# Graph attention on one core: which PSUM bank holds what, and the order of the readers of PE

## The chip, the core and the metric

The kernel runs on one core of one Trainium2 chip. The metric is the device time in microseconds. Three runs of the kernel before give a median of 2156.45 us (2150.37 to 2159.99).

## What is computed

A graph has N = 12500 nodes with 128 features and E = 212500 edges, sorted by their destination, each with 128 features of its own. There are 8 heads of 16 features.

```python
Q, K, V = x @ WQ, x @ WK, x @ WV            # (N, 8, 16) each
Eh = edge_attr @ WE                          # (E, 8, 16)
score = K[src] * Q[dst] / sqrt(16) * Eh
score = exp(clip(score.sum(-1), -5, 5))      # (E, 8, 1)
wV = segment_sum(V[src] * score, dst)        # (N, 8, 16)
Z = segment_sum(score, dst)                  # (N, 8, 1)
h = x + (wV / (Z + 1e-6)).reshape(N, 128)
h = (h - mean(h)) * rsqrt(var(h) + 1e-5) * gamma + beta   # over the nodes
out = layernorm(x + h)                       # over the features, no weights
```

## The kernel before

**Tiles.** Edges lie in tiles of 128, one per partition. A group holds two windows of 4 tiles; the last group holds 3 and 2. There are 208 groups (`NG`). Since the edges are sorted, the destinations of one window fall into 64 consecutive nodes, which begin at `BASE[g][h]`. `hx` holds x, transposed, in SBUF for the whole run; it is overwritten by h as groups end.

**Head.** PE multiplies x with the K and V weights, and the products go to a table `kvd` in DRAM (`table_rows`, L605). The first 8 groups don't wait for this table: for them GpSimd gathers rows of x (64 gathers), and K and V are computed on the spot, for groups 0 to 3 during the head, for groups 4 to 7 in the main loop (`project_main`, L277 and L284). All others take their rows of K and V from `kvd`: 1585 indirect DMAs on GpSimd's queue (L198), one for each tile, into 8 slots that hold one group each. The message of a group frees its slot. In 12 groups one tile is instead fetched row by row from SyncE's queue (L231). Gathers are let go one by one: `pace` makes a gather wait for a certain DVE instruction, seven in each group, and an eighth goes when a slot comes free.

**One group in the main loop.** The order in which the functions are called is the order on each engine, as nothing is scheduled by a tool (`manual_schedule`). For group g:

- `ehqe` (two groups ahead): PE computes Eh (L500, bank `ps_e`) and Q at the edges (L503, bank `ps_q`): Q is split into three bf16 parts and multiplied with a one-hot matrix. ACT copies Eh to SBUF (L506).
- `both` (one ahead): DVE multiplies the two (L512). `turn_back`: PE transposes the product (L520, `ps_t`).
- `products`: DVE multiplies by K (L529); `scores` adds up 16 features of a head (L536); `clip_exp` clips (L541), and ACT writes the exponential twice, to PSUM for DVE (L543) and to SBUF (L544).
- `onehot` (L460 to L463): DVE compares node numbers with an iota that lies in PSUM. `message` (L550): DVE multiplies V by the exponential.
- `gather_sum` (one behind): PE adds the messages of each node by the one-hot (L565), with a carry from the window before (L564). `sums_out`: ACT copies the sums (L570).
- `denom`, `recip`, `attn` (two behind): DVE divides (L574, L577, L581). `add_x`: PE turns the result and adds x (L587, L588), ACT writes it to `hx` (L590). `bn_part`: statistics over nodes (L593).
- `q_window`, `q_mm`, `q_hi`, `q_mid`, `q_lo` (two to four ahead): ACT cuts 64 nodes out of `hx` (L449), PE computes Q (L480), ACT and DVE split it (L484, L488, L489, L492).

**Banks.** PSUM has 8 banks here: two each of `ps_e`, `ps_q` and `ps_t`, one `ps_m` (`small_ps`) and one `ps_a` (`sum_ps`). `ps_m` holds Q in two alternating places, the update of x, and a place for odd jobs. `ps_a` holds the sums, the iota and the exponentials of two groups. Semaphores guard a bank as a whole: an instruction that reads or writes it waits for those of other engines that touched the bank before it.

**End.** After the loop, which runs two rounds past the last group for its updates, `norm_factors` makes scale and shift (`ab`). All engines then come to a branch (L724): if the input doesn't fit the assumptions, a slow path (`any_order`) is computed instead; here it is skipped. Then comes the last stage, 25 tiles of 512 nodes: `residual` (h scaled and shifted, plus x; DVE at L764, or GpSimd, tile 0 on DVE, L767 and L768), `centred` (PE turns the tile and subtracts the mean, L776 and L778), `variance` (ACT, Square with a sum for each block of 128 nodes, L796, or bn_stats on DVE for three tiles, L791 and L793; square root on ACT, L798), `scaled` (DVE, L806 and L812; output on SyncE's queue, L814).

Of the kernel before, what the change touches and what calls it, by code (L numbers as in the profile page):

```python
# [17 lines left out]
H = 8  # L18
# [44 lines left out]
def gnn_kernel(  # L63
# [41 lines left out]
    small_ps = psp.tile([P, 4, P], F32, name="ps_m", bufs=1)  # L105


    sum_ps = psp.tile([P, 4 * P], F32, name="ps_a", bufs=1)
    iota_ps = sum_ps[:, W:W + P]

    def exp_ps(g):
        c = W + P + (g % 2) * G * H
        return sum_ps[:, c:c + G * H].rearrange("p (t h) -> p t h", h=H)
# [46 lines left out]
    iota = consts.tile([P, P], F32, name="iota")  # L160
    nc.vector.tensor_copy(iota, io_i)
# [4 lines left out]
    nc.vector.tensor_scalar(ident, iota, piota, None, op0=OP.is_equal)  # L166
# [6 lines left out]
    nc.vector.memset(ones, 1.0)  # L173
    eps = consts.tile([P, 1], F32, name="eps")
# [151 lines left out]
    def place(r):  # L326
        nc.vector.tensor_copy(vw(rel, r), vw(rel_i, r))
        nc.vector.tensor_tensor(vw(rel, r), vw(rel, r), bc(base_f, r), op=OP.subtract)
        end = ustarts[r[0]] + (r[1] - r[0]) * r[2]
        for t in range(ustarts[r[0]], end, P):  # L330
            n = min(P, end - t)
            ps = small_ps[:, 3, :]
            nc.tensor.transpose(ps[:n], rel[:, t:t + n], ident)
            row = wp.tile([P, P], BF16, name="relrow", bufs=2)
            nc.vector.tensor_copy(row[:n], ps[:n])
            nc.scalar.dma_start(relT[t:t + n, :], row[:n])
# [22 lines left out]

    def shift_tiles():  # L360

        t = rows.tile([P, 4, 2 * P], F32, name="t", bufs=4)
        shift3, rows3 = t[:, 0, :65], t[:65, 1, :P // 2].bitcast(BF16)
        nc.vector.memset(rows3, 0.0)
        nc.vector.memset(shift3, 0.0)
        for r in (0, 32, 64):
            nc.vector.memset(rows3[r:r + 1, :], 1.0)
        return rows3, shift3
# [5 lines left out]
    def check(i):  # L374
# [17 lines left out]
        elif i == len(runs) + 1:  # L392
# [4 lines left out]
            ps = small_ps[:, 3, :]  # L397
# [45 lines left out]
    def q_window(g):  # L443
# [3 lines left out]
        XW[g] = wp.tile([P, P], F32, name="xw", bufs=7)  # L447
# [30 lines left out]
    def q_mm(g):  # L478
        PQ[g] = small_ps[:, g % 2, :]
        nc.tensor.matmul(PQ[g], XW[g], w_q, start=True, stop=True)  # L480
# [13 lines left out]
    def ehqe(g):  # L494

        QE[g], WT[g] = [], []
        for h, (a, b) in enumerate(halves(g)):
            eh = psp.tile([P, U * P], F32, name="ps_e", bufs=2)[:, :(b - a) * P]
            qe = psp.tile([P, U * P], F32, name="ps_q", bufs=2)[:, :(b - a) * P]
            nc.tensor.matmul(eh, w_e, EA[g][:, a:b, :].rearrange("p a b -> p (a b)"), start=True, stop=True)  # L500
            r = slice(h * WN, (h + 1) * WN)
            for k in range(3):
                nc.tensor.matmul(qe, Q3[g][r, k, :], OT[g][r, :(b - a) * P], start=(k == 0), stop=(k == 2))  # L503
            QE[g].append(qe)
            t = wp.tile([P, U * P], F32, name="wt", bufs=2)
            nc.scalar.activation(t[:, :(b - a) * P], eh, AF.Copy)  # L506
            WT[g].append(t)

# [30 lines left out]
    def clip_exp(g):  # L539
# [5 lines left out]
        if g == NG - 1:  # L545
            nc.scalar.activation(warm, eps, AF.Sqrt)
# [38 lines left out]
    def add_x(g):  # L585
        ps = small_ps[:, 2, :]
        nc.tensor.matmul(ps, AT[g], ident, start=True, stop=False)  # L587
        nc.tensor.matmul(ps, ident, XW[g], start=False, stop=True)  # L588
        for h in (0, 1):
            nc.scalar.activation(hx[:, ds(BASE[g][h], WN)], ps[:, h * WN:(h + 1) * WN], AF.Copy)  # L590
# [67 lines left out]
    ehqe(1)  # L658
    within(load, 2)
# [11 lines left out]
    for g in range(NG + 2):  # L671
# [5 lines left out]
        within(both_halves, g + 1)  # L677
        within(gather_sum, g - 1)
        within(q_mm, g + 3)
        within(scores, g)  # L680
        within(clip_exp, g)
        within(sums_out, g - 1)
        within(q_hi, g + 3)
# [4 lines left out]
        if g + 1 < nxg and g + 1 not in SLOT:  # L688
            for _ in project_main(g + 1):
                pass  # L690
        within(turn_back, g + 1)
        within(add_x, g - 2)
        within(q_window, g + 4)
        within(turned_onehot, g + 3)
        within(onehot, g)
        within(ehqe, g + 2)
        within(message, g)
        within(q_mid, g + 3)
# [9 lines left out]
        if g == NG // 2:  # L708
            three = shift_tiles()
# [3 lines left out]
        for w in (2 * g - 3, 2 * g - 2):  # L713
            for j in due.get(w, []):
                bn_part(j)
                done.add(j)
    for j in range(NCH):
# [6 lines left out]
    with tc.If(flag[0] != 0):  # L724
        any_order(tc, N, T, hx, xT, src, dst, eaT, w_q, w_e, kvd, dram, ident, stats, cuts)
        norm_factors()


    fin = ctx.enter_context(tc.tile_pool(name="fin", bufs=3))
    fps = ctx.enter_context(tc.tile_pool(name="fps", bufs=8, space=bass.MemoryType.PSUM))  # L730
    Y, PY, V = {}, {}, {}
# [3 lines left out]
    if len(pairs[-1]) > 1 and width(NY - 1) < B4:  # L735
        pairs[-1:] = [[NY - 2], [NY - 1]]

# [4 lines left out]
    rows3, shift3 = three  # L742


    nc.vector.tensor_copy(shift3[:, 0:65:32], ab[:, 1:2].to_broadcast([P, 3]))
    row_ps = fps.tile([P, 4, P], F32, name="ps_y", bufs=8)[:65, 0, :]
    nc.tensor.matmul(row_ps, shift3, cent, start=True, stop=True)
    row = fin.tile([65, P], BF16, name="row", bufs=1)
    rest = fin.tile([65, P], F32, name="rest", bufs=1)

    def shift_row():
        nc.vector.tensor_copy(row, row_ps)  # L752
        nc.vector.tensor_sub(rest, row_ps, row)
        nc.vector.tensor_copy(row[32:33], rest[32:33])
        nc.vector.tensor_copy(row[64:65], rest[64:65])
        nc.vector.tensor_sub(row[64:65], rest[64:65], row[64:65])

    def residual(i):

        c, n = i * B4, width(i)  # L760
        Y[i] = fin.tile([P, B4], F32, name="y", bufs=6)
        y, h = Y[i][:, :n], hx[:, c:c + n]
        if i in on_vector:
            nc.vector.scalar_tensor_tensor(y, h, ab[:, 0:1], XR[i][:, :n], op0=OP.mult, op1=OP.add)  # L764
        else:
            eng = nc.gpsimd if i else nc.vector
            eng.tensor_scalar(y, h, ab[:, 0:1], ab[:, 1:2], op0=OP.mult, op1=OP.add)  # L767
            eng.tensor_tensor(y, y, XR[i][:, :n], op=OP.add)  # L768
        if i == 0:
            shift_row()  # L770

    def centred(i):
        PY[i] = fps.tile([P, 4, P], F32, name="ps_y", bufs=8)
        whole = i in on_vector
        if whole:
            nc.tensor.matmul(PY[i], rows3, row[:, None, :].to_broadcast([65, 4, P]), start=True, stop=False)  # L776
        for k, m in blocks(i):
            nc.tensor.matmul(PY[i][:m, k, :], Y[i][:, k * P:k * P + m], cent, start=not whole,  # L778
                             stop=(k == 3 or not whole))

    def variance(p):
        v = fin.tile([P, 2, 4, 2], F32, name="v", bufs=4)
        V[p[0]] = v
        sq = fin.tile([P, P], F32, name="sq")
        if blocks(p[-1])[-1][1] < P:
            nc.vector.memset(v, 1.0)
        for h, i in enumerate(p):
            if i in by_stats:
                bn = fin.tile([P, 4, 6], F32, name="bn", bufs=2)
                for k in range(4):  # L790
                    nc.vector.bn_stats(bn[:, k, :], PY[i][:, k, :])  # L791
                for k in range(4):
                    nc.vector.bn_aggr(v[:, h, k, :], bn[:, k, :])  # L793
            else:
                for k, m in blocks(i):
                    nc.scalar.activation(sq[:m], PY[i][:m, k, :], AF.Square, scale=P ** -0.5,  # L796
                                         accum_out=v[:m, h, k, 1:2])
        nc.scalar.activation(spread(p), spread(p), AF.Sqrt, bias=eps)  # L798

    def spread(p):  # L800
        nb = len(blocks(p[-1]))
        return V[p[0]][:, :len(p), :nb, 1]

    def scaled(p):
        v = V[p[0]]
        nc.vector.reciprocal(spread(p), spread(p))  # L806
        o = fin.tile([P, 2, 4, P], F32, name="o")
        for h, i in enumerate(p):
            bl = blocks(i)
            c, fb = i * B4, sum(m == P for _, m in bl)  # L810
            if fb:
                nc.vector.tensor_tensor(o[:, h, :fb, :], PY[i][:, :fb, :],  # L812
                                        v[:, h, :fb, 1:2].to_broadcast([P, fb, P]), op=OP.mult)
                nc.sync.dma_start(out[c:c + fb * P, :].rearrange("(c p) d -> p c d", p=P), o[:, h, :fb, :])  # L814
            for k, m in bl[fb:]:
                nc.vector.tensor_scalar(o[:m, h, k, :], PY[i][:m, k, :], v[:m, h, k, 1:2], None, op0=OP.mult)
                nc.sync.dma_start(out[c + k * P:c + k * P + m, :], o[:m, h, k, :])

    on_vector = {i for i in range(2, NY, 2) if width(i) == B4}
    by_stats = {i for i in range(5, NY, 8) if width(i) == B4}  # L820
    for i in range(len(pairs) + 4):
        for f, k in ((residual, i), (centred, i - 1), (variance, i - 1), (scaled, i - 2)):
            if 0 <= k < len(pairs):
                if f in (residual, centred):
# [136 lines left out]
```

## Time and profile before

| what | value |
|---|---|
| median of three runs | 2156.45 us |
| profiled execution, whole | 2865.58 us |
| its span, first to last instruction | 2863.8 us |
| granted clock of PE, mean | 0.804 |
| DMA, mean rate | 135 GB/s |
| groups of the main loop | 208 |
| first products (L529) | at 101.2 us |
| last products | at 2795.1 us |
| gathers from `kvd` (L198) | 1585, 949 ns each, first at 106.8 us |

In the prediction's lines, a group stands as: line, engine, operation, output<-inputs, shape, count, then busy time and mean duration, then idle time of the engine just before these instructions and what ended most of it. In a timeline the first number is the start in us from the span's begin, the second the duration, and the bracket holds idle time before it and its releaser. In the table by stretches, each row has the stretch, its length, then the busy time of PE, weight loads (PEld), DVE, ACT and POOL (GpSimd), with counts, then granted clock, DMA share and GB/s. PE's ends are modelled, its starts are recorded.

### The profile page before, as it was taken

Reading aid. Unit: us, or ns where it says so; the run is one execution under the profiler, and the core shown is the slowest. Engines: PE = TensorE matmul, PEld = TensorE weight load, DVE = VectorE, ACT = ScalarE, POOL = GpSimd, SP = SyncE. Lnnn points to the kernel's source line nnn. Section 1 sums busy time; section 2 is a strip of 40 time slices with the busy share of each in tenths; the row PEclk is TensorE's granted clock in tenths of the full one; section 3 lists DMA queues with packets and bytes.
Section 4 is the critical chain, followed back from the end, with each engine's and each line's share of the span. In section 5 each row is a group of like instructions: output and inputs, shape, how many; then the busy total and the mean of one; then the engine's idle time right before and its main releaser. Section 6 shows DMA issues by size and latency. Waiting matters only on the chain. (4 is left out here: it accounts for less than half of the span.)

```text
span 2863.8 us, 37931 instructions
## 1 busy us (share of the span) xinstructions
PE 2215.0 (77%) x9339; PEld 1237.7 (43%) x9339; DVE 1666.6 (58%) x3597; ACT 683.0 (24%) x2539; POOL 1594.8 (56%) x1681
## 2 busy tenths in 40 slices
PE   7778778867787777877778777877877777877895
PEld 6444444433443443444434444433434444444454
DVE  3346556555655655655556655555555565656586
ACT  2132222222222222222222222222222222222235
POOL 6634555555555555555556555565556555655524
PEclk8788777788868878788987778788788787878797
DMA  7643444444444444444444444444444444444353
GB/s 244 200 122 115 132 118 144 131 136 124 134 115 137 135 135 131 135 120 130 127 136 129 135 126 137 128 137 126 128 133 138 127 139 134 126 144 130 115 178 94
DMA packets 179738, 386.84 MB, mean 135 GB/s; under 512 B 41838, under 2 KB 96151, under 8 KB 179511
## 3 DMA queue, kind: packets, MB, share of 16 engines
q0 software_dynamic: 78128, 212.05, 25.7%
q1 hardware_dynamic: 98038, 169.83, 19.3%
q10 hardware_dynamic: 3345, 2.48, 0.3%
q8 instruction: 77, 1.26, 0.2%
q14 instruction: 150, 1.23, 0.1%
HBM read 364.57 MB, written 19.63 MB: 134 GB/s over the span
## 5 line engine op out<-in xcount | busy, mean ns | idle before, releaser
L198 POOL DMA_INDIRECT slot<-kvd,srcs x1585 | 1504.1, 949 | 1137.2 <-DVE oh L463 322.2
L565 PE MATMUL ps_a<-msg,oh 128*128 128x136 f32 (+1 forms) x3322 | 643.1, 341 | 17.0 <-issue 11.7
L500 PE MATMUL ps_e<-ea,w_e 128*128 128x512 f32 x832 | 598.6, 810 | 2.5 <-DMA ea<-eaT 2.5
L565 PEld LDWEIGHTS ps_a<-msg,oh 128*128 128x128 f32 (+1 forms) x3322 | 501.4, 195 | 221.3 <-issue 173.7
L512 DVE TENSOR_TENSOR wt<-wt,ps_q 128x512 f32<-128x512 f32 x416 | 279.3, 683 | 375.7 <-remote 123.5
L587 PE MATMUL ps_m<-ident,at 128*128 128x128 f32 x416 | 120.6, 380 | 439.5 <-ACT q L484 281.0
L503 PE MATMUL ps_q<-ot,q 64*128 64x512 bf16 x1248 | 433.8, 465 | 0.0
L460 DVE TENSOR_TENSOR oh<-ps_a,rel_i 128x512 f32<-128x512 f32 x208 | 142.7, 686 | 444.9 <-ACT os L570 329.2
L506 ACT ACTIVATE wt<-ps_e 128x512 f32<-128x512 f32 x416 | 242.3, 591 | 396.9 <-PE ps_e L500 215.3
L520 PE MATMUL ps_t<-ident,wt 128*128 128x128 f32 x1661 | 239.8, 288 | 103.8 <-DVE wt L512 97.3
L503 PEld LDWEIGHTS <-q 64*128 64x128 bf16 x1248 | 96.0, 104 | 516.1 <-issue 485.6
L543 ACT ACTIVATE ps_a<-s 128x64 f32<-128x64 f32 x208 | 47.4, 228 | 1101.0 <-remote 555.3
L587 PEld LDWEIGHTS ps_m<-ident,at 128*128 128x128 f32 x416 | 78.5, 236 | 480.0 <-ACT q L484 315.0
L529 DVE TENSOR_TENSOR p<-slot,ps_t 128x512 f32<-128x512 f32 (+1 forms) x408 | 257.6, 672 | 11.2 <-remote 10.6
L536 DVE TENSOR_REDUCE s<-p 128x64 f32<-128x1024 f32 x208 | 251.5, 1209 | 0.0
L520 PEld LDWEIGHTS ps_t<-ident,wt 128*128 128x128 f32 x1661 | 198.7, 148 | 118.8 <-DVE wt L512 109.0
L550 DVE TENSOR_TENSOR msg<-slot,ps_a 128x1024 f32<-128x1024 f32 (+1 forms) x204 | 244.6, 1199 | 0.0
L500 PEld LDWEIGHTS ps_e<-ea,w_e 128*128 128x128 f32 x832 | 160.4, 240 | 123.9 <-issue 120.3
L590 ACT ACTIVATE hx<-ps_m 128x64 f32 x416 | 93.6, 225 | 436.1 <-PE ps_m L588 153.2
L488 DVE SCALAR_TENSOR_TENSOR qr<-ps_m,q 128x128 f32<-128x128 f32 x208 | 59.3, 285 | 224.2 <-ACT hx L590 208.6
L449 ACT ACTIVATE xw<-hx 128x64 f32 x416 | 84.1, 248 | 92.4 <-ACT hx L590 66.6
L588 PE MATMUL ps_m<-xw,ident 128*128 128x128 f32 x416 | 103.0, 339 | 0.0
(119 smaller groups left out, 1584.5 us busy)
## 6 DMA issues: line engine op xcount, KB each, us to landing
ea<-eaT SPq DMA_DIRECT2D x207, 512.0 KB
rb<-relT SPq DMA_DIRECT2D x414, 64.0 KB
slot<-kvd,srcs POOLq DMA_INDIRECT x1585
byrow<-kvd SPq DMA_DIRECT2D x1536, 1.0 KB
kvd<-t SPq DMA_DIRECT2D x24, 512.0 KB
slot<-xT SPq DMA_DIRECT2D x24, 256.0 KB
out<-o SPq DMA_DIRECT2D x24, 256.0 KB
hx<-xT SPq DMA_DIRECT2D x11, 512.0 KB
```

The lines of the kernel that those rows point to most:

```text
L198: return nc.gpsimd.indirect_dma_start(out=out, out_offset=None, in_=table, in_offset=bass.IndirectOffsetOnAxis(ap=srcs[:, e:e + 1], axis=0))
L460: nc.vector.tensor_tensor(one, iota_ps[:, None, :].to_broadcast([P, n, P]), r[:, :n, None].to_broadcast([P, n, P]), op=OP.is_equal)
L500: nc.tensor.matmul(eh, w_e, EA[g][:, a:b, :].rearrange("p a b -> p (a b)"), start=True, stop=True)
L503: nc.tensor.matmul(qe, Q3[g][r, k, :], OT[g][r, :(b - a) * P], start=(k == 0), stop=(k == 2))
L506: nc.scalar.activation(t[:, :(b - a) * P], eh, AF.Copy)
L512: pace(nc.vector.tensor_tensor(t, t, QE[g][h], op=OP.mult))
L520: nc.tensor.transpose(ps[:, j, :], WT[g][h][:, j * P:(j + 1) * P], ident)
L529: step = nc.vector.tensor_tensor(PR[g][:, c:d, :], KV[g](c, d, 0), PW[g][i][:, c - a:d - a, :], op=OP.mult)
L536: pace(nc.vector.tensor_reduce(SS[g][:, :n, :], PR[g][:, :n, :].rearrange("p t (h d) -> p t h d", d=DH), axis=AX.X, op=OP.add))
L550: nc.vector.tensor_tensor(MSG[g][:, a:b, :P].rearrange("p t (h d) -> p t h d", d=DH), KV[g](a, b, P).rearrange("p t (h d) -> p t h d", d=D ...
L565: nc.tensor.matmul(AGG[g][WN if j >= n else 0:], OH[g][j], MSG[g][:, j, :], start=(j == 0), stop=(j == n - 1))
L587: nc.tensor.matmul(ps, AT[g], ident, start=True, stop=False)
```

## The change

In PSUM, iota and exponentials move from `ps_a` to `ps_m`, and the odd jobs from `ps_m` to `ps_a`; Q has one place instead of two, next to the update of x. `ps_a` then holds only the sums and, seldom, an odd job. The calls in the loop get another order. `add_x` is cut in two (PE's part and ACT's part, `x_out`) and comes a group later, at the head of the round; `onehot` is one group ahead, after the message; `project_main` and `turn_back` come before the scores; the sums' copy comes after Q's copy. `ehqe` issues both Eh products first. The two rounds past the last group are replaced by updates written out. The last stage is made a function that runs before the branch, and again inside it if the slow path was taken. In it, tile 0 is computed in two halves on ACT and DVE, eight tiles have their squares added by DVE (`by_reduce`) and none uses bn_stats, and the shift row is one fp32 row instead of three bf16 ones.

```diff
-    iota_ps = sum_ps[:, W:W + P]
+    iota_ps, spare_ps = small_ps[:, 2, :], sum_ps[:, W:W + P]
     def exp_ps(g):
-        c = W + P + (g % 2) * G * H
-        return sum_ps[:, c:c + G * H].rearrange("p (t h) -> p t h", h=H)
+        c = (g % 2) * G * H
+        return small_ps[:, 3, c:c + G * H].rearrange("p (t h) -> p t h", h=H)
...
-        XW[g] = wp.tile([P, P], F32, name="xw", bufs=7)
+        XW[g] = wp.tile([P, P], F32, name="xw", bufs=8)
...
-        PQ[g] = small_ps[:, g % 2, :]
+        PQ[g] = small_ps[:, 0, :]
...
-        for h, (a, b) in enumerate(halves(g)):
+        for a, b in halves(g):
             eh = psp.tile([P, U * P], F32, name="ps_e", bufs=2)[:, :(b - a) * P]
-            qe = psp.tile([P, U * P], F32, name="ps_q", bufs=2)[:, :(b - a) * P]
             nc.tensor.matmul(eh, w_e, EA[g][:, a:b, :].rearrange("p a b -> p (a b)"), start=True, stop=True)
-            r = slice(h * WN, (h + 1) * WN)
-            for k in range(3):
-                nc.tensor.matmul(qe, Q3[g][r, k, :], OT[g][r, :(b - a) * P], start=(k == 0), stop=(k == 2))
-            QE[g].append(qe)
             t = wp.tile([P, U * P], F32, name="wt", bufs=2)
             nc.scalar.activation(t[:, :(b - a) * P], eh, AF.Copy)
             WT[g].append(t)
+            QE[g].append(psp.tile([P, U * P], F32, name="ps_q", bufs=2)[:, :(b - a) * P])
+        for k in range(3):
+            for h, (a, b) in enumerate(halves(g)):
+                r = slice(h * WN, (h + 1) * WN)
+                nc.tensor.matmul(QE[g][h], Q3[g][r, k, :], OT[g][r, :(b - a) * P], start=(k == 0), stop=(k == 2))
...
     def add_x(g):
-        ps = small_ps[:, 2, :]
+        ps = small_ps[:, 1, :]
         nc.tensor.matmul(ps, AT[g], ident, start=True, stop=False)
         nc.tensor.matmul(ps, ident, XW[g], start=False, stop=True)
+
+    def x_out(g):
+        ps = small_ps[:, 1, :]
         for h in (0, 1):
             nc.scalar.activation(hx[:, ds(BASE[g][h], WN)], ps[:, h * WN:(h + 1) * WN], AF.Copy)
...
-    for g in range(NG + 2):
+    for g in range(NG):
         within(load, g + 4)
         within(load_rel, g + 5)
         if g in fill:
             fetch_rows(*fill[g])
         within(products, g)
         within(both_halves, g + 1)
+        within(add_x, g - 3)
+        within(q_mm, g + 3)
         within(gather_sum, g - 1)
-        within(q_mm, g + 3)
+        if g + 1 < nxg and g + 1 not in SLOT:
+            for _ in project_main(g + 1):
+                pass
+        within(turn_back, g + 1)
         within(scores, g)
         within(clip_exp, g)
+        within(q_hi, g + 3)
+        within(x_out, g - 3)
         within(sums_out, g - 1)
-        within(q_hi, g + 3)
         within(q_lo, g + 2)
         within(denom, g - 2)
         within(recip, g - 2)
         within(attn, g - 2)
-        if g + 1 < nxg and g + 1 not in SLOT:
-            for _ in project_main(g + 1):
-                pass
-        within(turn_back, g + 1)
-        within(add_x, g - 2)
         within(q_window, g + 4)
         within(turned_onehot, g + 3)
-        within(onehot, g)
         within(ehqe, g + 2)
+        within(q_mid, g + 3)
+        if g == NG - 1:
+            add_x(g - 2)
+            x_out(g - 2)
+            update(g - 1)
+            nc.scalar.activation(warm, eps, AF.Sqrt)
         within(message, g)
-        within(q_mid, g + 3)
+        within(onehot, g + 1)
...
-        for w in (2 * g - 3, 2 * g - 2):
+        for w in range(2 * g - 5, 2 * g + 1 if g == NG - 1 else 2 * g - 3):
...
+    gather_sum(NG - 1)
+    sums_out(NG - 1)
+    update(NG - 1)
...
+    by_reduce = {i for i in range(3, NY, 2) if width(i) == B4 and i % 6 != 1}
...
+            if i == 0:
+                for a in range(0, n, 2 * P):
+                    b = min(n, a + 2 * P)
+                    nc.scalar.activation(y[:, a:b], h[:, a:b], AF.Identity, scale=ab[:, 0:1], bias=ab[:, 1:2])
+                    nc.vector.tensor_tensor(y[:, a:b], y[:, a:b], XR[i][:, a:b], op=OP.add)
+                nc.vector.tensor_copy(row, row_ps)
...
+                if i in by_reduce:
+                    sq4 = fin.tile([P, 4, P], F32, name="sq4", bufs=2)
+                    nc.scalar.activation(sq4, PY[i], AF.Square, scale=P ** -0.5)
+                    nc.vector.tensor_reduce(v[:, h, :, 0], sq4, axis=AX.X, op=OP.add)
...
+    finish()
     with tc.If(flag[0] != 0):
         any_order(tc, N, T, hx, xT, src, dst, eaT, w_q, w_e, kvd, dram, ident, stats, cuts)
         norm_factors()
+        finish()
```

In the changed kernel `update(g)` calls `denom`, `recip`, `attn`, `add_x` and `x_out` for one group. One-hot is at L451 there, the exponential at L534, the sums at L554.

## The prediction

> **What bounds the kernel now.** First the page's busy times, then the groups. No engine is full: PE 77%, DVE 58%, POOL 56%. But this profiled execution took 2865.6 us (span 2863.8, 1.8 around it) and the median of the runs is 2156.45, so 709 us of the profile are not in the runs. I must find out which rows are real.
>
> ```profile
> PE 2215.0 (77%) x9339; PEld 1237.7 (43%) x9339; DVE 1666.6 (58%) x3597; ACT 683.0 (24%) x2539; POOL 1594.8 (56%) x1681
> ...
> L198 POOL DMA_INDIRECT slot<-kvd,srcs x1585 | 1504.1, 949 | 1137.2 <-DVE oh L463 322.2
> ...
> L460 DVE TENSOR_TENSOR oh<-ps_a,rel_i 128x512 f32<-128x512 f32 x208 | 142.7, 686 | 444.9 <-ACT os L570 329.2
> ...
> L587 PE MATMUL ps_m<-ident,at 128*128 128x128 f32 x416 | 120.6, 380 | 439.5 <-ACT q L484 281.0
> ```
>
> The timelines of PE and ACT around 1220 us show what is not real. PE's last sum matmul starts at 1217.87 and should be over by 1218.4, DVE's clip ends at 1217.9, yet the exponential that waits for both starts at 1222.35, "remote". In this stretch the register rows of SyncE, elsewhere 0.04 us, take 0.70 us each.
>
> ```profile
> 1217.87 0.50 PE L565 MATMUL ps_a<-msg,oh 128*128 128x136 f32 x2
> ...
> 1223.14 0.49 PE L587 MATMUL ps_m<-ident,at 128*128 128x128 f32 x2 [3.69 <-ACT q L484]
> ```
> ```profile
> 1222.35 0.23 ACT L543 ACTIVATE ps_a<-s 128x64 f32<-128x64 f32 x1 [9.03 <-remote]
> ```
>
> 77 such stalls before L543 sum to 555 us. I take them for the price of recording (inferred: all sequencers are slow at once, and without them the time comes near the runs'). What an undisturbed group costs is read where there are none:
>
> ```profile
> 236.38 2.03 PE L565 MATMUL ps_a<-msg,oh 128*128 128x136 f32 x14
> ...
> 239.22 1.04 PE L520 MATMUL ps_t<-ident,wt 128*128 128x128 f32 x8
> 240.10 0.39 PE L587 MATMUL ps_m<-ident,at 128*128 128x128 f32 x2
> ...
> 244.06 1.22 PE L565 MATMUL ps_a<-msg,oh 128*128 128x136 f32 x7
> ```
> ```profile
> 2724.69 0.95 POOL L198 DMA_INDIRECT slot<-kvd,srcs  x1 [0.30 <-issue]
> ...
> 2727.20 0.95 POOL L198 DMA_INDIRECT slot<-kvd,srcs  x1 [0.30 <-issue]
> ```
>
> PE needs 7.68 us per group, without a gap (236.38 to 244.06); DVE 7.47 (1201.32 to 1208.79). A gather starts 1.254 us after the one before it even when nothing holds it (0.95 busy, 0.30 to the next), and none of the 1585 starts closer than 1.24. Eight make 10.03 us per group. So without the stalls GpSimd's gathers set the pace, PE and DVE wait 2.3 us per group for landings.
>
> The sum: products of group 0 start at 101.2 us. Groups 0 to 7 free only the slots of 64 gathers, so gather 64 waits for the messages of group 8; it starts at 242.48, after 13.56 us of waiting. Undisturbed, four of these groups take 7.68 us and the four with a projection 13.07 (206.78 to 219.85 on PE); with 7.4 to the end of message 8 that is 101.2 + 30.7 + 52.3 + 7.4 = 191.6. Then 1521 gathers x 1.254 = 1907.3. Landing (2.4 us after issue, from the DMA packets of three lone gathers) adds 1.1, the last group's start 0.8, the way from its products to the end 68.7 (2795.1 to 2863.8), the rest 1.8: 2171, 0.7% above the median. That fits, so I forecast differences and take them off 2156.
>
> **The change part by part.**
>
> *Banks and order in the loop.* Sums get bank ps_a alone; iota, exponentials, Q and x's update share ps_m; the one-hot of g+1 comes after message g; x's update runs three groups late, at the head of PE's group. The one-hot no longer waits for the sums' copy (L460 <- ACT L570, 329 us), PE no longer for Q's copy inside the group (L587 <- ACT L484, 281 us). The Trainium skill ("PSUM — Partial Sum Buffer", section on bank collisions) says that two engines must not touch one bank at once, so accesses are guarded by bank and not by address. By that rule the bank that is split pays: 329 us, 11% of the profiled time. By the row of the gathers it pays nothing, since a group lasts 10.03 us anyway. I take 0. New waits: at the head of its group, PE waits for DVE's one-hot (same bank), and sums, turn-back and Eh/QE are queued behind it, 7.68 us of PE. DVE reaches that point 7.5 us after a landing, inside the 10.03, so 2.3 us of cover hide it; without cover, it would be up to 1.3 us (the one-hot: 0.69 + 0.23 + 0.42, overlapped) per group. Both Eh products now precede the six QE ones, and bn_stats run one group later: the same rows in the same cover, 0. SyncE's loads and row fetches keep their place, and GpSimd's gathers stay tied to the same DVE steps.
>
> *Start.* Until gather 64 the groups themselves set the time. Message 8 now stands ahead of a one-hot: 1.3 us. The projections come before the exponentials, so that ACT's copies don't queue behind them; on PE these groups have gaps of 0.3 us undisturbed, 4 to 5 us twice (180.3, 199.1). Bounds 0 and 20; nearest the undisturbed row: 1 us. Together -2.3.
>
> *End of the loop.* DVE's chain:
>
> ```profile
> 2795.11 0.86 DVE L529 TENSOR_TENSOR p<-slot,ps_t 128x384 f32<-128x384 f32 x2
> ...
> 2801.15 0.56 DVE L460 TENSOR_TENSOR oh<-ps_a,rel_i 128x384 f32<-128x384 f32 x1 [3.34 <-ACT os L570]
> ...
> 2808.14 0.32 DVE L593 BATCH_NORM_STATS2 stats<-hx 128x6 f32<-128x148 f32 x1 [4.47 <-ACT hx L590]
> ...
> 2811.36 0.86 DVE L353 BATCH_NORM_AGGREGATE mv<-stats 128x2 f32<-128x156 f32 x1
> ...
> 2816.41 0.17 DVE L745 COPY t<-ab 128x3 f32<-128x3 f32 x1 [3.08 <-DVEq L724]
> ```
>
> Now the last message starts 7.0 us after its products (2802.08), behind exponential, Sqrt table (1.28), copy and one-hot (1.07). After, one-hot and table are out of its way, but two updates stand in it, and the message waits for the second's copies (same bank): about 4.2 for attn 206, 1.3 for PE, 0.7 for two copies: 6.2, so -0.8. Then statistics (0.32) and update 206 no longer stand between the last sums and the last update: -1.6. The branch, 3.08 us, moves behind the last stage: -3.1, and +1 there, since DVE takes it while SyncE's last output still lands. Sum -4.5. Bounds: 0 if the new waits eat all but the branch, -8 if the message needn't wait.
>
> *Last stage.* ACT sets it:
>
> ```profile
> 2846.00:2854.00 8.00, 6.61 (x54) 5.83 (x54) 6.64 (x19) 7.41 (x41) 3.62 (x4) 1.00 0.61 183
> ```
>
> In this row of the table by stretches the fourth busy time is ACT's: 7.41 of 8, the rest the gaps between its rows. A full tile costs ACT 4 x 0.40 us, 21 of them 33.7. After, 16 cost that (25.7) and 8 one 512-wide Square, 0.59 by the nearest row (wt<-ps_e) and 0.03 gap: 5.0. That is -3.0 on ACT. DVE loses three tiles of bn_stats (1.15 each) and the split of the shift row (2.4), gains eight reduces (0.65, half of the 1024-wide 1.21): -0.7, near 33 of the 38 us, so waits between the two will take about half: -1.5, bounds 0 and -3. The first tile in two halves on ACT and DVE instead of 2.3 us of DVE (2817.10 to 2819.38): -1.7, bounds -2 and 0. Sum -3.2. The small ones (one iota copy, a memset, the fp32 row) are under 0.3.
>
> All: -2.3 - 4.5 - 3.2 = -10.0, so 2146. In the profiled execution the stalls may fall anywhere: its loop can move by 100 us either way and prove nothing about the runs.
>
> **Rivals.**
> 1. *As summed:* 2146, 0.66; own range 2137 to 2155. For it: the 1.254 us that never shrink, and a sum within 0.7% of the median.
> 2. *The start gives more.* If the runs too have PE gaps of 4 to 5 us in all four projecting groups, they go: -18 more, 2128, 0.12. Against: 180 to 200 us is a disturbed stretch.
> 3. *The gap of 0.30 us is recording as well,* and the runs are bound by the waits. (2156 - 192 - 72)/200 = 9.5 us per group now, about 8.2 after (DVE's 7.5 and the new guard): -260, 1896, 0.10. This is the change doing all it says. Against: groups of 7.68 us exist with the old order.
> 4. *Slower: PE's clock.* The skill ("TensorE: Matmul & The Clock Gate", HAM part) halves PE's clock after an idle window of about 3.4 us. Now PE's 2.3 idle us per group lie in two places (turn-back and L587); after the change they lie in one, before the turn-back. The trace: clock 0.97 from 2750 to 2800 us where PE is dense, 0.80 over all, with idle times of 3.7 us. By the rule alone 2.3 is under the window and costs nothing; by the trace's mean clock, 7.68/0.80 = 9.6, still under 10.03. It decides below 7.68/10.03 = 0.77: at 0.75 a group takes 10.24, +0.21 x 190 = +40, 2186. Chance 0.12.
>
> **Numbers.** Chances 0.66, 0.12, 0.10, 0.12. The range takes in rivals 1 and 2 and leaves the others out: 2125 to 2157. A measurement here tells about 0.5% (10.8 us) from no change. Of rival 1 some 0.28 lies beyond 10.8 us, 0.38 within; with rivals 2 and 3: faster 0.50, same 0.39, slower 0.11 (a part of rival 4 stays under 10.8 us).
>
> **What would show it.** Right: gathers again 1.25 us apart; no wait of L451 for ACT; no 3 us branch between the last aggregate and the last stage; products to end near 61 us instead of 68.7; ACT near 34 us in the last stage. Wrong: gathers much closer than 1.25, a time under 2100 (rival 3), or a granted clock below 0.77 with PE waiting in one place (rival 4).

## The result, and the profile after

The changed kernel takes 2151.64 us (median of 8 runs, 2148.92 to 2156.02), the kernel before 2158.8 beside it (8 runs): a ratio of 0.997, 95% interval 0.9959 to 0.9981. That is 7 us, or 0.3%: a gain, but smaller than the 0.5% that the prediction set as its bound. 2146 was forecast, with a range of 2125 to 2157.

The first profile of before was a disturbed execution (span 2863.8 us). The kernel before was therefore profiled again, unchanged, as `before_again`: span 2155.9 us, granted clock 0.910. All comparisons of traces below use that one. The changed kernel's span is 2147.0, clock 0.941, and 1.9 us lie around it; this traced execution is the fastest of its eight.

> The kernel before, unchanged, for a trace without the stalls of the first one. If gathers set the pace: starts 1.25 us apart from gather 64 on with under 15 us of waits in all, DVE waiting for landings in some 150 groups, span near 2155; gather 64 about 2 us later than after the change (171.5), and 67 to 69 us from the last products to the end. If the runs are bound by the waits between PE, ACT and DVE: gathers with waits of several us in each group, as in the first trace.

Measured: 2157.75 us. The 77 stalls are gone with the disturbed execution. Gathers start 1.25 us apart, as expected if they set the pace; but gather 64 starts 7.4 us later than in the changed kernel (178.9 against 171.5), not 2.

The page of the changed kernel:

```profile
PE 1681.1 (78%) x9350; PEld 1094.9 (51%) x9350; DVE 1640.5 (76%) x3571; ACT 630.7 (29%) x2509; POOL 1592.5 (74%) x1681
...
L199 POOL DMA_INDIRECT slot<-kvd,srcs x1585 | 1502.9, 948 | 490.4 <-issue 202.0
...
L520 DVE TENSOR_TENSOR p<-slot,ps_t 128x512 f32<-128x512 f32 (+1 forms) x408 | 272.6, 677 | 356.1 <-DMA slot<-kvd,srcs 328.4
...
L576 PE MATMUL ps_m<-ident,at 128*128 128x128 f32 x416 | 101.6, 328 | 320.2 <-DVE oh L454 313.0
...
L498 PE MATMUL ps_q<-ot,q 64*128 64x512 bf16 x1248 | 171.2, 380 | 0.0
L451 DVE TENSOR_TENSOR oh<-ps_m,rel_i 128x512 f32<-128x512 f32 x208 | 141.8, 682 | 0.0
```

And of `before_again`:

```profile
PE 1906.4 (88%) x9339; PEld 1105.7 (51%) x9339; DVE 1653.6 (77%) x3597; ACT 675.3 (31%) x2539; POOL 1593.3 (74%) x1681
...
L503 PE MATMUL ps_q<-ot,q 64*128 64x512 bf16 x1248 | 371.0, 408 | 0.0
...
L587 PE MATMUL ps_m<-ident,at 128*128 128x128 f32 x416 | 99.8, 325 | 136.8 <-DVE at L581 121.3
...
L460 DVE TENSOR_TENSOR oh<-ps_a,rel_i 128x512 f32<-128x512 f32 x208 | 142.0, 683 | 39.7 <-ACT os L570 38.7
```

Three things stand in these rows. The one-hot (L451) waits for nobody any more; in the undisturbed profile that wait was only 38.7 us, not the 329 of the first one. PE now waits 313 us for the one-hot, at the head of its group (L576), where before it waited 121.3 us for DVE's `at`. And a row that the prediction doesn't have: the products of Q with the one-hot, the same 1248 instructions of nearly the same mean length (408 and 380 ns), keep PE busy for 171 us instead of 371.

Where the 9 us between the two spans lie:

| stretch | before_again | after |
|---|---|---|
| first products to gather 64 | 96.6 us | 88.9 us |
| gather 64 to the last gather | 1905.0 | 1904.5 |
| last gather to the end | 72.0 | 70.9 |

The long middle, 1520 gathers 1.253 us apart, did not move. The start gave 7.7 us, the end 1.1.

### The profile page after: what moved, and what is told of

The parts are those of the page before. It is cut to its first block, busy times and chain, and to the rows that moved or that the text cites. A ratio compares the mean times of both kernels' runs of the same rounds, so it can differ in the third digit from the quotient of the medians.

```text
span 2147.0 us, 37902 instructions
## 1 busy us (share of the span) xinstructions
PE 1681.1 (78%) x9350; PEld 1094.9 (51%) x9350; DVE 1640.5 (76%) x3571; ACT 630.7 (29%) x2509; POOL 1592.5 (74%) x1681
## 3 DMA queue, kind: packets, MB, share of 16 engines
q14 instruction: 152, 1.25, 0.2%
## 5 line engine op out<-in xcount | busy, mean ns | idle before, releaser
L554 PE MATMUL ps_a<-msg,oh 128*128 128x136 f32 (+1 forms) x3322 | 570.1, 315 | 1.5 <-DVE msg L539 1.5
L554 PEld LDWEIGHTS ps_a<-msg,oh 128*128 128x128 f32 (+1 forms) x3322 | 463.5, 183 | 87.5 <-issue 65.3
L534 ACT ACTIVATE ps_m<-s 128x64 f32<-128x64 f32 x208 | 47.3, 227 | 1333.8 <-DVE s L532 1045.7
L490 PE MATMUL ps_e<-ea,w_e 128*128 128x512 f32 x832 | 404.8, 610 | 2.4 <-DMA ea<-eaT 2.1
L576 PE MATMUL ps_m<-ident,at 128*128 128x128 f32 x416 | 101.6, 328 | 320.2 <-DVE oh L454 313.0
L576 PEld LDWEIGHTS ps_m<-ident,at 128*128 128x128 f32 x416 | 66.1, 200 | 412.3 <-ACT q L480 359.5
L539 DVE TENSOR_TENSOR msg<-slot,ps_m 128x1024 f32<-128x1024 f32 (+1 forms) x204 | 244.7, 1200 | 1.6 <-ACT hx L582 1.4
L498 PE MATMUL ps_q<-ot,q 64*128 64x512 bf16 x1248 | 171.2, 380 | 0.0
L451 DVE TENSOR_TENSOR oh<-ps_m,rel_i 128x512 f32<-128x512 f32 x208 | 141.8, 682 | 0.0
L498 PEld LDWEIGHTS <-q 64*128 64x128 bf16 x1248 | 44.1, 94 | 186.4 <-issue 161.7
L570 DVE SCALAR_TENSOR_TENSOR at<-os,keep,rz 128x128 f32<-128x128 f32 x208 | 73.2, 352 | 24.4 <-DVE rz L566 0.9
L471 PE MATMUL ps_m<-w_q,xw 128*128 128x128 f32 x416 | 88.4, 297 | 1.6 <-ACT xw L440 0.9
```

Of the source, the lines that this page charges most:

```text
L451: nc.vector.tensor_tensor(one, iota_ps[:, None, :].to_broadcast([P, n, P]), r[:, :n, None].to_broadcast([P, n, P]), op=OP.is_equal)
L498: nc.tensor.matmul(QE[g][h], Q3[g][r, k, :], OT[g][r, :(b - a) * P], start=(k == 0), stop=(k == 2))
L539: nc.vector.tensor_tensor(MSG[g][:, a:b, :P].rearrange("p t (h d) -> p t h d", d=DH), KV[g](a, b, P).rearrange("p t (h d) -> p t h d", d=D ...
L554: nc.tensor.matmul(AGG[g][WN if j >= n else 0:], OH[g][j], MSG[g][:, j, :], start=(j == 0), stop=(j == n - 1))
```

## The experiments

All times are medians; each ratio is to the kernel before, run beside it (its medians: 2158.2, 2162.7 and 2159.2). The theory that came out of the prediction was: gathers set the pace of the loop, so banks and orders are worth only what they do in the start, and the rest comes from the end.

**Do gathers set the pace?** In 12 groups SyncE fetches one tile row by row, and GpSimd has a gather fewer. Here one such group is left.

```diff
-    return [2 * g for g in range(max(FIRST_ROW + span, NX), sizes.count(U) // 2, P // ROWS)]
+    return [2 * g for g in range(max(FIRST_ROW + span, NX), sizes.count(U) // 2, P // ROWS)][:1]
```

> The changed kernel with one group instead of 12 whose last tile SyncE fetches row by row, so 11 gathers more on GpSimd and 1408 small DMAs less on SyncE. If gathers set the pace: 11 x 1.2525 = +13.8 us, so 2165. If PE, DVE or ACT do: 0 or a little below.

Measured: 2166.07, ratio 1.0037 (1.0027 to 1.0048), 14.4 us above the changed kernel. 11 more gathers at 1.2525 us are 13.8. Gathers set the pace.

**Which half holds the gain: the loop or the end?** One kernel has the loop of before and the end of after (everything from the normalizing factors on, with the branch behind the last stage), the other the loop of after (from banks to the last update) and the end of before.

> The loop of before with the end of after (last stage ahead of the branch, squares by reduce, shift row in one piece). If only start and end count: -5 us of the -7 (ratio 0.9977). If the order in the loop brings the gain: 0 to -1 us.

> The loop of after, its banks and order, with the branch and the last stage of before. If only start and end count: -2 us (ratio 0.999), from the start and the last updates. If the order in the loop brings the gain: -6 to -7 us.

Measured: end alone 2159.75, ratio 1.0009 (1.0001 to 1.0017); loop alone 2150.97, ratio 0.9966 (0.9952 to 0.9979). In both runs the first theory (only start and end count: -5 and -2 us) fails, in opposite directions, and the other one comes out: the new end gains nothing, it costs about 2 us, and the whole gain, 7.3 us, is in the loop's code.

**Is it the banks?** The kernel before with only the places in PSUM changed:

```diff
-    iota_ps = sum_ps[:, W:W + P]
+    iota_ps, spare_ps = small_ps[:, 2, :], sum_ps[:, W:W + P]
...
-        c = W + P + (g % 2) * G * H
-        return sum_ps[:, c:c + G * H].rearrange("p (t h) -> p t h", h=H)
+        c = (g % 2) * G * H
+        return small_ps[:, 3, c:c + G * H].rearrange("p (t h) -> p t h", h=H)
...
-        PQ[g] = small_ps[:, g % 2, :]
+        PQ[g] = small_ps[:, 0, :]
```

> Kernel before with only the banks changed: iota and exponentials share the small bank with Q and the update of x, the sums of a group have their bank for themselves; every order, the copy of iota, and the whole end stay as before. Before is about 2158. The traces show the start 7.4 us earlier after the change, 5.0 of it in groups 0 and 1. T1 (the bank: in before exp(1) waits until PE has done sums(0), which lie in its bank): 5 us faster, about 2153, groups 0 and 1 together take 16 us instead of 21, gather 64 starts near 173.5 instead of 178.9. T2 (the order alone: the message ahead of the one-hot, PE's work moved): no change, 2157 to 2159, gather 64 near 178.9.

Measured: 2169.11, ratio 1.0037 (1.0023 to 1.0052): 8 us slower by the ratio, 6.4 by the medians. My explanation (the exponential of group 1 waits for PE's sums in its bank) fell. DVE's timeline of this kernel shows what the banks do without the orders:

```profile
200.58 0.43 DVE L470 TENSOR_SCALAR ot<-rb,wiota 128x512 bf16<-128x512 bf16 x1
202.04 0.69 DVE L460 TENSOR_TENSOR oh<-ps_m,rel_i 128x512 f32<-128x512 f32 x1 [1.03 <-ACT hx L590]
```

The one-hot only reads the iota, but the iota now shares a bank with the update of x, so DVE waits 1.03 us until ACT has copied that update out; over the whole run these waits are 295.0 us in 206 groups. A group that isn't held by gathers takes 8.64 us instead of 7.67 (products to products). Gather 64 starts at 187.4 instead of 178.9.

**Is it the order of Q's products?** PE's timeline of one group, first `before_again`:

```profile
192.34 1.02 PE L500 MATMUL ps_e<-ea,w_e 128*128 128x512 f32 x2
193.30 0.82 PE L503 MATMUL ps_q<-ot,q 64*128 64x512 bf16 x3
194.05 1.12 PE L500 MATMUL ps_e<-ea,w_e 128*128 128x512 f32 x2
195.11 0.82 PE L503 MATMUL ps_q<-ot,q 64*128 64x512 bf16 x3
195.85 2.03 PE L565 MATMUL ps_a<-msg,oh 128*128 128x136 f32 x14
```

and then the changed kernel:

```profile
184.39 1.88 PE L490 MATMUL ps_e<-ea,w_e 128*128 128x512 f32 x4
186.21 0.82 PE L498 MATMUL ps_q<-ot,q 64*128 64x512 bf16 x6
187.78 0.46 PE L576 MATMUL ps_m<-ident,at 128*128 128x128 f32 x2 [0.74 <-DVE oh L454]
```

Three products of one half take 0.82 us; six, the two halves in turn, take 0.82 as well. One half reads partitions 0 to 63, the other 64 to 127. That the pair runs side by side stands in the recorded starts as well: in the changed kernel they come in pairs, 0.003 us apart within a pair and some 0.22 us from pair to pair (186.208 and 186.211, 186.435 and 186.438, 186.650 and 186.654); in `before_again` each product starts some 0.22 us after the one before it. The Trainium skill ("TensorEngine Tiling (Array Packing)", Key Properties under Tiling Modes) says that different tiles of the array can multiply in parallel; its table under Theoretical Speedup puts the gain for a dimension of at most 64 at up to 2, which is what the rows give. Two kernels test what this is worth: before with the new order of these products alone (both Eh products ahead, then the six in turn), and after with the old one.

```diff
-        for h, (a, b) in enumerate(halves(g)):
+        for a, b in halves(g):
...
-            r = slice(h * WN, (h + 1) * WN)
-            for k in range(3):
-                nc.tensor.matmul(qe, Q3[g][r, k, :], OT[g][r, :(b - a) * P], start=(k == 0), stop=(k == 2))
...
+        for k in range(3):
+            for h, (a, b) in enumerate(halves(g)):
+                r = slice(h * WN, (h + 1) * WN)
+                nc.tensor.matmul(QE[g][h], Q3[g][r, k, :], OT[g][r, :(b - a) * P], start=(k == 0), stop=(k == 2))
```

> Kernel before with one thing of the change: Eh of both halves first, then the six matrix products of Q with the one-hot, part by part, the two halves in turn (banks, order and end as before). In the trace of after, six such products take PE 0.82 us, as long as three of one half take in before, so PE's work in a group falls from 7.67 us to about 6.7. T1 (this is what shortened the start, where groups set the time and PE is the bound, in groups 0 and 1 at half clock): groups 0 and 1 together 17 to 18 us instead of 21, the projecting groups 12.5 instead of 13.1, gather 64 near 173 instead of 178.9, 2151 to 2153 where before is 2158. T2 (banks and order did it): 2157 to 2159.

> Kernel after with that one thing undone: each half's Eh is followed by its own three products of Q with the one-hot (banks, order and end as after). T1 (the halves in turn shortened the start): PE's group is 7.7 us again and now also waits 0.7 us at its head for the one-hot, so 8.3 us a group where PE sets the time; gather 64 near 180 instead of 171.5, 2158 to 2162. T2 (banks and order did it): 2151 to 2153.

Measured: together in before 2149.81, ratio 0.9962 (0.9948 to 0.9976); apart in after 2161.7, ratio 1.0003 (0.9993 to 1.0013). These few lines alone are worth 8 us, and without them the whole change is worth nothing that the runs can tell. Gather 64 starts at 168.4 and 178.6 us (173 and 180 were expected).

Where do the 8 us lie? The start is 8.6 us shorter in `halves_together` than in `before_again`: 4.5 of them in groups 0 and 1, 3.5 in groups 2 to 6 (a projecting group takes 12.2 us instead of 13.1), 0.6 after that. In groups 2 to 6 the granted clock is 1.00 in both, so there the gain is PE's shorter group. In groups 0 and 1 it is 0.67 in `before_again` and 1.00 in `halves_together`; in the undisturbed traces it is 0.67 to 0.71 in the five kernels with the halves apart (17.8 to 22.0 us for the two groups) and 0.80 to 1.00 in the eight with the halves in turn (15.2 to 16.7). So about half of the gain comes with a clock that stays up. How the order brings that about was not tested.

**And the order without the banks?** The kernel after, with iota and exponentials back in the bank of the sums (the diff of the banks, reversed).

> Kernel after with the banks of before: iota and exponentials lie in the bank of the sums, Q in two places, the order and the end as after. The other half to the run that changed the banks alone and lost 6 us. T1 (the orders already keep the readers of PE's banks apart; the split of banks adds nothing here): 2150 to 2154, catching-up groups 7.5 us. T2 (banks and order only pay together, the exponential waits again for PE's sums): 7.9 us or more for a catching-up group, gather 64 near 176, 2155 to 2159.

Measured: 2147.05, ratio 0.9943 (0.9929 to 0.9956). Even the first theory was too mild: the split of the banks not only adds nothing, it costs some 5 us in the runs, 2.6 of which the traces show in the start (86.3 us, against 87.8 to 90.4 in the six traces with the new banks and the halves in turn); where the rest lies is not shown. This is the fastest kernel of the study; its interval doesn't meet that of the changed kernel. A projecting group takes 12.1 us in it, 12.7 in the changed kernel. The first line of PE's group shows the difference; in `order_alone`:

```profile
129.54 0.49 PE L576 MATMUL ps_m<-ident,at 128*128 128x128 f32 x2
```

and in the changed kernel:

```profile
131.98 0.46 PE L576 MATMUL ps_m<-ident,at 128*128 128x128 f32 x2 [0.76 <-DVE oh L454]
```

With the iota in the other bank PE need not wait for the one-hot before it turns the update.

The start in all of these traces, from first products to gather 64:

| kernel | banks | order | halves in turn | start | time - before |
|---|---|---|---|---|---|
| before_again | old | old | no | 96.6 us | 0 |
| banks_alone | new | old | no | 104.2 | +8 |
| halves_together | old | old | yes | 88.0 | -8 |
| halves_apart | new | new | no | 94.0 | +1 |
| order_alone | old | new | yes | 86.3 | -12 |
| after | new | new | yes | 88.9 | -6.5 |

The last column is the ratio less one, times the median of before. The starts follow the times to within some 4 us; what is left is not accounted for piece by piece.

**What are these orders worth where gathers don't bind?** From group 16 on, half of each group's gathers become one plain load. These two kernels change part of the computation: the edges concerned read the first rows of the table instead of their own nodes' K and V.

```diff
-            for j in range(sizes[g] - (g in by_row)):
+            m = sizes[g] - (g in by_row)
+            k = m - m // 2 if g >= nxg + NSLOT else m
+            if k < m:
+                nc.sync.dma_start(KV[g](k, m, 0, 2 * P), kvd[:(m - k) * P, :].rearrange("(a p) d -> p a d", p=P))
+            for j in range(k):
```

> Kernel before with, from group 16 on, half of the gathers of each group (3 or 4 of 8) replaced by one plain load by SyncE of as many tiles of K and V from the table's first rows, so these edges don't read their own nodes' K and V. It takes the gathers off the pace of the loop. T1 (gathers set the pace, and behind them the waits between PE, ACT and DVE hold 7.7 to 8.0 us a group): 1700 to 1760 us. T2 (the engines' waits set the pace already, gathers merely keep up): above 2050.

> Kernel after with the same replacement of half of the gathers from group 16 on (those edges read the table's first rows). It shows what the order of the loop and the banks are worth where gathers don't set the pace. T1 (the new order and banks save PE-ACT-DVE waits that gathers hide at present): 0.2 to 0.6 us for each of some 190 groups less than the same edit of before, 40 to 110 us. T2 (the order of the loop is worth nothing by itself): within 10 us of the same edit of before.

Measured: 1815.13 with the old loop (ratio 0.8383, 0.836 to 0.8405) and 1792.04 with the new one (0.8292, 0.8279 to 0.8305). Gathers do set the pace. Both expectations of the totals fail: the 7.91 us a group in the old loop is inside the expected 7.7 to 8.0, but 236.4 us up to group 16, 191 times 7.91 and 66 from there to the end make 1814, not 1700 to 1760. The difference of 23 us (25 in the traces) lies between the two expectations, 8 of it ahead of gather 64, 17 in 191 groups: 0.09 us each. The table by stretches, for 200 us of the old loop and then of the new:

```profile
1000.00:1200.00 200.00, 199.16 (x1086) 117.52 (x1084) 194.17 (x424) 73.11 (x281) 97.48 (x103) 0.99 0.66 210
```
```profile
1000.00:1200.00 200.00, 176.27 (x1086) 114.17 (x1084) 193.12 (x423) 70.65 (x280) 96.99 (x103) 0.99 0.66 211
```

PE falls from 199 to 176, DVE (third busy time) stays at 193 to 194 of 200. DVE is next in line, which fits that PE's saving is nearly all given back.

**Why does the new end gain nothing?** In the changed kernel's last stage PE is full. Its table by stretches:

```profile
2107.40:2118.00 10.60, 10.60 (x63) 7.26 (x61) 8.47 (x16) 8.33 (x41) 7.05 (x7) 1.00 0.50 142
2118.00:2128.00 10.00, 10.00 (x61) 7.19 (x61) 8.75 (x17) 8.37 (x42) 7.39 (x8) 1.00 0.67 185
```

and that of `before_again`:

```profile
2134.00:2144.00 10.00, 7.50 (x58) 6.11 (x57) 8.83 (x16) 9.24 (x52) 6.50 (x7) 1.00 0.58 169
```

PE's busy time, the first, went from 7.5 of 10 to 10 of 10, while ACT's (the fourth) fell from 9.24 to 8.37. The row that adds the shift accounts for it, L772 of the changed kernel, here at half and at full clock:

```profile
2099.19 2.07 PE L772 MATMUL ps_y<-row,ones_row 1*128 1x512 f32 x2
...
2108.03 1.12 PE L772 MATMUL ps_y<-row,ones_row 1*128 1x512 f32 x2
```

and the same of `before_again`, as three bf16 rows:

```profile
2115.34 0.38 PE L776 MATMUL ps_y<-row,t 65*128 65x512 bf16 x1
```

A single fp32 row counts as two records and takes 1.12 us at full clock, as long as an Eh product of 128 fp32 rows (1.02 to 1.12 above); three bf16 rows take 0.38. Eleven tiles have such a row: 8 us of PE. The test is the kernel after with the bf16 rows back:

```diff
-        row_ps = fps.tile([P, 4, P], F32, name="ps_y", bufs=8)[0:1, 0, :]
-        nc.tensor.matmul(row_ps, ab[:, 1:2], cent, start=True, stop=True)
-        row = fin.tile([1, P], F32, name="row", bufs=1)
+        nc.vector.tensor_copy(shift3[:, 0:65:32], ab[:, 1:2].to_broadcast([P, 3]))
+        row_ps = fps.tile([P, 4, P], F32, name="ps_y", bufs=8)[:65, 0, :]
+        nc.tensor.matmul(row_ps, shift3, cent, start=True, stop=True)
+        row = fin.tile([65, P], BF16, name="row", bufs=1)
...
-                nc.tensor.matmul(PY[i], ones_row, row[:, None, :].to_broadcast([1, 4, P]), start=True, stop=False)
+                nc.tensor.matmul(PY[i], rows3, row[:, None, :].to_broadcast([65, 4, P]), start=True, stop=False)
```

> Kernel after with the shift row of the last stage as before the change: three bf16 rows in 65 partitions instead of one float32 row. T1 (the float32 row costs PE 1.12 us for each of 11 tiles against 0.38, and PE is busy all the time in the last stage of after): 11 x 0.74 = 8 us less of PE; ACT and DVE are then next with 8.8 us of each 10, so about 4 us faster than after, 2147.5, and first Square to last output 38 to 39 us instead of 42.8. T2 (what lengthens the last stage is DVE's reduce of the squares or the order of the pairs): 2151 to 2153, no change, and PE simply waits more.

Measured: 2153.33, ratio 0.9964 (0.995 to 0.9977), against 0.997 for the changed kernel: the intervals overlap, so the runs don't decide. The trace does in part. PE is no longer full:

```profile
2109.50:2119.50 10.00, 7.59 (x58) 6.03 (x56) 9.49 (x17) 8.73 (x45) 8.00 (x8) 1.00 0.57 169
```

and from the first Square to the last output 38.5 us go by instead of 42.8, as before the change (38.4). The other traces agree, and they show how much this stretch varies. With the fp32 row this stretch follows PE's granted clock: 39.7 and 39.8 us at 0.97 (`order_alone`, `half_after`), 42.4 to 42.8 at 0.90 (`fewer_rows`, `halves_apart`, `after`), 45.2 at 0.84 (`end_alone`). With the bf16 rows it hardly does: 38.4 to 38.6 at 0.90 to 0.94 in six traces, 40.2 at 0.88 in a seventh (`more_rows_bf16`). So at the same clock, 0.90, the fp32 row costs some 4 us; at 0.97 it is still 1.3 us above the 38.4 of the bf16 rows.

The way to the factors also hangs on that clock. From the last gather to the end, four traces of the old end give 71.5 to 73.4 us, five of the new one with its fp32 row 70.9 to 80.1 (the 80.1 is that of the slowest of `end_alone`'s 13 executions). In the changed kernel the last full group's sums took

```profile
2079.86 1.93 PE L554 MATMUL ps_a<-msg,oh 128*128 128x136 f32 x14
```

and in `halves_apart`, the same instructions:

```profile
2089.00 3.57 PE L554 MATMUL ps_a<-msg,oh 128*128 128x136 f32 x14
```

The granted clock there is 1.00 in the first and 0.65 in the second, and from the last group's products to the last step of the factors 13.7 and 17.8 us went by. At equal clock (0.59 to 0.60 over this stretch) the old loop takes 18.5, 18.7 and 18.0 us (`before_again`, `end_alone`, `halves_together`), the new one 17.5, 17.4 and 17.8 (`fewer_rows`, `loop_alone`, `halves_apart`): the new code gains about 0.8 us there, and the rest of the 4.8 between `before_again` and the changed kernel comes with the clock.

**Fewer gathers still?** Since gathers set the pace, SyncE is given 24 tiles instead of 12, two rows' worth of steps in a group, with the bf16 rows of the run above.

```diff
-    return [2 * g for g in range(max(FIRST_ROW + span, NX), sizes.count(U) // 2, P // ROWS)]
+    return [2 * g for g in range(max(FIRST_ROW + span, NX), sizes.count(U) // 2, P // ROWS // 2)]
...
-            fetch_rows(*fill[g])
+            for f in fill[g]:
+                fetch_rows(*f)
```

> Kernel after with two things: SyncE fetches 24 tiles of K and V row by row instead of 12 (two rows' worth at a time), so GpSimd has 12 gathers fewer; and the shift row of the last stage as three bf16 rows. T1 (gathers set the pace; SyncE has room, with some 4.7 us of its own work in each 10 us group): 12 x 1.2525 = 15 us less, and 1 to 4 us less at the end, 2133 to 2136. T2 (SyncE's 16 row fetches a group come late and delay the loads of relT and edge features): 2145 or more.

Measured: 2278.19, ratio 1.0552 (1.0538 to 1.0566), 126 us slower than the changed kernel. SyncE's timeline shows why:

```profile
701.46 0.36 SPq L426 DMA_DIRECT2D ea<-eaT  x1
701.91 1.09 SPq L352 DMA_DIRECT2D rb<-relT  x2
704.22 7.48 SPq L238 DMA_DIRECT2D byrow<-kvd  x16
711.80 0.36 SPq L426 DMA_DIRECT2D ea<-eaT  x1
```

From one load of edge features to the next, the queue needs 10.34 us without waiting for anything: 16 rows 0.41 us apart in two steps, about 1 us ahead of each step for the load of its row numbers (0.99 and 0.79 here), and the loads of the group. That is more than the 10.02 of the gathers, and from there the group's loads come late. The waits of this kernel:

```profile
DVE ot L467 <- DMA rb<-relT: 444.7, 172, 3.9
PE ps_e L496 <- DMA ea<-eaT: 326.9, 164, 3.8
```

and SyncE's own wait ahead of the loads of edge features, in this kernel and then in the changed one, where it still has time to spare:

```profile
SPq L426 <- PE ps_e L496: 40.9, 9, 11.7
```
```profile
SPq L420 <- PE ps_e L490: 608.8, 168, 11.7
```

The step of my estimate that failed is SyncE's 4.7 us a group: with the load of the row numbers it is nearer 6, and another 4.3 on top fill the group. Why 126 us, when the queue is only 0.3 us too slow for a group of eight gathers? From group 16 to 207 a group takes 10.36 us here, the queue's own pace, but only 9.70 on average in the changed kernel, where the gathers of eight groups lie ready at gather 64 and groups 8 to 27 take 7.8 us each. 191 times 0.66 is 126.

## Why the prediction was right, and where it was not

The time, -7 us for -10 forecast, and the range hold. What carried it is the pace of the gathers, which leaves the loop unchanged. That the sum came near is luck: the start gave far more than forecast, for a reason that the sum had put at 0, and the end far less.

- *Gathers set the pace of the loop, its banks and orders are worth 0 there.* Right: 1905.0 and 1904.5 us. The stalls before L543 are not in the runs, as the prediction said; but they belong to that one execution and are not the price of recording, since `before_again` was recorded too and has none. The base sum (2171) came 15 us above the median because it took the head of the disturbed trace: first products at 101.2 us, 82.4 undisturbed. The forecast was a difference from the median, so this did no harm.
- *New wait at the head of PE's group, hidden by 2.3 us of cover.* Right: 313 us of L576 waiting for the one-hot, and no time lost under the gathers. Where there is no cover, in the projecting groups, PE waits 0.5 to 0.76 us a group for it; the prediction named up to 1.3 for that, but did not charge it to the start.
- *"The same rows in the same cover, 0"*, for both Eh products ahead of the six QE ones. This step failed. The rows are the same in number and nearly in length, not in their overlap: about 0.8 us of PE a group disappear. Under the gathers that is indeed 0; in the start, where groups set the time, it is 8.6 us (`halves_together`), half of them in groups 0 and 1, where the clock differs too.
- *Start -2.3* (message ahead of the one-hot, projections early). The orders and banks without the halves in turn give -2.6 (`halves_apart`), so the number fits; but with the halves in turn the same orders and banks give +0.9 (88.0 to 88.9), and the banks a loss of 2.6 (88.9 against 86.3 in `order_alone`), so the parts don't add up and the fit proves little. The start as a whole gave -7.7.
- *End of the loop -4.5.* Mis-sized. Products to factors went from 18.5 to 13.7 us in the two traces, but most of that comes with the clock; at equal clock it is about -0.8 for the -2.4 forecast. The branch left the path (2.8 us of waiting on DVE are gone) and came back at the end: from the last output to the end of the span 3.4 us became 6.6, +3.2 instead of the +1 that was allowed. The prediction counted DVE's way through the branch alone. But SyncE reaches it (L830) only behind its last output, at 2142.14, and its next instruction starts at 2144.71. So moving the branch gained nothing.
- *Last stage -3.2.* First tile -1.2 for -1.7; the rest +4.4 for -1.5. The step that failed is "the small ones (..., the fp32 row) are under 0.3": the row is 8 us of PE, costs 1 to 4 us of time by the traces, and makes PE full. ACT became lighter as forecast (busy for 31.6 us of the stage instead of 34.4). The check that the prediction named, products to end near 61 us, gives 67.4 instead.
- *Rivals.* A start that gives more (2128): half right, for a reason that the prediction didn't have. The gap of 0.30 us as a matter of recording (1896): refuted, the traces whose spans fit the runs have the same 1.253, and 11 gathers more cost 14.4 us in the runs. A slower clock (2186): refuted, it rose from 0.91 to 0.94 in the traces. None of the rivals was that the banks themselves cost time, and this is what the runs show.

What stays open: whether the bf16 rows gain anything in the median (the traces say 1 to 4 us in the last stage, the runs can't tell), how the order of Q's products keeps the clock up in groups 0 and 1, where 2 to 3 us of the banks' loss lie, and what the old banks and the old end give together with the new orders, which wasn't run.

## What to carry to other kernels

Where one resource sets the pace of a loop, edits to the other engines show only outside of it, in ramps and tails: cost each edit there, by those stretches' own bound. Before an instruction's reordering is put at nothing, look whether its neighbours use different parts of the same array, and where a whole bank is the unit of waiting, judge a move by who writes into the new bank. Before work is moved to a queue, add up all that it issues in a period, the loads of its registers too.

## What the runs showed of the hardware

- Six bf16 products that use 64 partitions each, the two halves of the partitions in turn, took PE 0.82 us, as long as three of one half; their starts come in pairs 0.003 us apart.
- A product with one fp32 row, 512 wide, took 1.12 us at full clock and 2.07 at half; with 65 partitions of bf16 it took 0.38.
- PE's clock differs between traces in the same stretch (1.00 and 0.65 in the last full group), and the way from the last products to the factors differs with it (13.7 and 17.8 us).
- A branch that all engines come to cost 2.8 us of waiting on DVE in front of the last stage; at the end of the kernel 2.6 us went by on SyncE between it and the next instruction.
